# Edge items held behind the middle stage on DVE and ACT, and the diagonal written from another queue: a four-layer graph network on one core

## The chip, the cores and the metric

The kernel runs on one core of a Trainium2 chip. The metric is the device time of one execution in microseconds; the time before is the median of three runs. A core has five engines with a queue each: TensorE (PE, with its weight loads PEld), VectorE (DVE), ScalarE (ACT), GpSimd (POOL) and SyncE (SP). SP issues DMA transfers alone; POOL issues the indirect ones (gathers and scatters by a list of indices) and some plain ones.

## The reference, cut to what matters

32 graphs of 512 nodes with 256 features go through four layers, all in float32. The adjacency matrix is shared by all graphs and sparse: a bernoulli mask of 1/128, made symmetric, with the diagonal set.

```python
# layers 0 and 3, with weights of their own
hidden = relu(pre_u[:, :, None, :] + pre_v[:, None, :, :] + b1)      # pre_u = h W1[:d], pre_v = h W1[d:]
S = sigmoid(einsum('buvk,ko->buvo', hidden, W2)[..., 0] + b2[0])
a_t = einsum('buv,bud->bvd', S * A_a, h_t)
m_t = einsum('uv,bud->bvd', A_m, h_t) * h_t
z_t = beta1 * h_t + beta2 * (a_t Wa + ba) + beta3 * (m_t Wm + bm)
# layer 1
z + relu((A z) W^T + b)
# layer 2
feats = data W1^T;  f1 = feats W2 + b2
coefs = softmax(leaky_relu(f1_i + f1_j) + bias1)                     # bias1 is the adjacency matrix
coefs feats + bias2 + data
```

S is needed only where the adjacency matrix is not zero: at the edges and on the diagonal.

## The kernel before

**Groups, edges and items.** Where no node has too many neighbours (the case here), `sparse_path` runs. The 32 graphs are taken in 8 groups of four (`NB`). For layers 0 and 3 the edges are packed beforehand into 36 lists of 128 edges (`ITEMS`), the same for all graphs. For each group and each of the two layers, a table in DRAM holds pre_u and pre_v of all nodes for the four graphs (`pre`, L547 to L555 write it: L547 adds the bias out of PSUM, L548 copies the other half on ACT, L550 and L551 make the diagonal's sums `self_s`, SP stores the result at L555). An edge stage (`edges`) then works through the 36 items: POOL gathers 128 rows of the table (`fetch`, L580, "rows<-table,iv"), SP or POOL brings the rows of the other end of the edges ("mine", L620 or L580), DVE adds the two (L652) and makes four reductions, one per graph (L665), into `s`. Every four items ACT takes exp (`exp_of`, L565), and DVE finishes the sigmoid and multiplies by the edge's value (`sigmoid_of`, L569 and L570, then L609). POOL scatters each finished list into `cells` in DRAM (`put`, L574), two halves of the matrix in turn; a scatter into a half waits for the one before it into that half. The diagonal (`own_1`) gets its exp after item 2 and its sigmoid after item 4, L600 multiplies it by the diagonal of the matrix, and POOL writes it into `cells` (L604). A stage fetches three items ahead (five at the program's ends) into five row buffers.

**The middle stage.** When a group's edge stage of layer 0 is through, four loads on POOL (`load`, L690) bring the cells back as SA, and `middle` takes the four graphs one after the other through the rest of layer 0 (L772 copies SA to `flat`; L713 mhT; L803 and L810 on PE, L808 and L811 give zT), layer 1 (L823 zW, L829 and L830 yT) and layer 2 (L841 feats, L845 fcol, L848 the transposes into f; the softmax in L856 to L862, its transposes L901 and the copies L902; L879 adds the result to yT), and then through layer 3's `pre`, which fills the table for layer 3's edge stage. When that has run, `last` makes the group's output (L703, L713, L943, L950, L959, L962).

**What sets the order.** `weave` writes the pieces of all stages of all groups into one list. Each stage is a generator, each `yield` ends a piece, and each piece has a due time in units of a group's period, set by hand in `sparse_path`; pieces are recorded in the order of their times. The stages overlap: while group t is in its middle stage, layer 3's edge stage of group t-1 runs in the first half of the period and layer 0's edge stage of group t+1 in the second half, and pieces of kind "fill" (`first`, which makes layer 0's table, and `last`) are put between the middle's pieces where these leave room. The recorded order is not the final one. When the program is built, a scheduler goes through it with its own estimate of durations, and on each engine it may put an instruction ahead of one recorded before it, if by that estimate the operands are there earlier. The order that it arrives at is fixed in the program; on the chip, DVE, ACT, POOL and SP work through their queues in it, and an instruction that waits holds up all behind it.

Of the kernel before, what the change touches and what calls it, by code (L numbers as in the profile page):

```python
# [11 lines left out]
AF = mybir.ActivationFunctionType  # L12
ALU = mybir.AluOpType
# [34 lines left out]
class Model:  # L48


    def __init__(self, ctx, tc, a):
        nc = self.nc = tc.nc
        self.tc, self.a = tc, a
        const = self.const = ctx.enter_context(tc.tile_pool(name="const", bufs=1))
        self.ident = const.tile([P, P], F32, name="ident")
        make_identity(nc, self.ident)
        self.adj = const.tile([P, NC, N], F32, name="adj")
        for c in range(NC):
            nc.sync.dma_start(self.adj[:, c, :], a["adj"][c * P : (c + 1) * P, :])
        self.g0, self.g3 = self.gnn_first("L0_gnn"), self.gnn_first("L3_gnn")  # L60
# [354 lines left out]
class Sparse:  # L415
# [3 lines left out]
    def __init__(self, ctx, m, counts, xr, outr, B):  # L419
        self.m, self.nc, self.tc, self.counts = m, m.nc, m.tc, counts  # L420
        tc = m.tc
        self.xr, self.outr = xr, outr
        pool = lambda n, b, **k: ctx.enter_context(tc.tile_pool(name=n, bufs=b, **k))
        self.dram = pool("dram", 1, space=bass.MemoryType.DRAM)

        self.cells = {
            k: [self.dram.tile([CELLS + SPARE, NB], F32, name=f"cells_{k}{q}") for q in range(2)] for k in "03"
        }
        self.lists = self.dram.tile([N, 2 * N], F32, name="lists")
        self.x2s = self.dram.tile([B, P, NC, D], F32, name="x2s")  # L430

        self.xT, self.x2T = (self.dram.tile([B, P, DC, N], F32, name=n) for n in ("xT", "x2T"))
        self.e = Edges(m, pool("edges", 1))
        self.adjT = pool("adjT1", 1).tile([P, NC, N], F32, name="adjT")
        self.grp = pool("grp", 2)
        self.act, self.small, self.gath = pool("act", 1), pool("small", 2), pool("gath", 5)
        self.ps = pool("ps", 7, space=PSUM)
        self.ps_f1 = pool("ps_f1", 1, space=PSUM)
        self.later, self.bigs, self.given = None, 0, None

    def psum(self):
        return self.ps.tile([P, N], F32, name="pst", tag="pst")
# [1 line left out]
    def weave(self, streams):  # L444

        order = []
        for k, (_, times, _) in enumerate(streams):
            order += [(at, k, j) for j, at in enumerate(times)]  # L450
        due, running = [], set()

        def run(k, j):
            g, times = streams[k][:2]
            room = next(g, None)
            if j == len(times) - 1:
                for _ in g:
                    raise AssertionError("more pieces than told")
            return room

        def fill(upto):
            while len(due) > upto:
                run(*due.pop(0))

        for _, k, j in sorted(order):
            kind, end = streams[k][2], len(streams[k][1]) - 1
            if kind == "fill":
                due.append((k, j))
                fill(HELD if running else 0)
                continue  # L470
            if kind == "main" and j == 0:
                running.add(k)
            elif j == 0 and kind != "free":
                fill(0)
            if run(k, j) and due:
                fill(len(due) - (1 if len(due) < HELD // 2 else 2))
            if kind == "main" and j == end:
                running.remove(k)
        fill(0)

    def big(self, dtype, n, layer=None):

# [79 lines left out]
        self.later = None  # L562

    def exp_of(self, w, t):
        self.nc.scalar.activation(t, t, AF.Exp, bias=w["nb2"], scale=-1.0)  # L565

    def sigmoid_of(self, t):

        self.nc.vector.tensor_scalar(t, t, 1.0, None, ALU.add)  # L569
        self.nc.vector.reciprocal(t, t)  # L570

    def put(self, g, half, at, s):
# [11 lines left out]
    def edges(self, g, spare=()):  # L584

        nc, e, w = self.nc, self.e, g.w
        flat = "p c b -> p (c b)"
        own = g.self_s.rearrange(flat)  # L590
        ready, fetched = [], {}
        lead = LEAD_AT_ENDS if spare else LEAD
        tags = [None] * 5 + list(spare)
        mine = {}
        places = g.table.rearrange("(c p k) n -> c k p n", p=P, k=2)

        def own_1():
            self.sigmoid_of(own)
            diag = self.counts.diag.unsqueeze(2).to_broadcast([P, NC, NB])
            nc.vector.tensor_tensor(g.self_s, g.self_s, diag, ALU.mult)  # L600
            for q in range(2):
                diagonal = g.cells[q][q * HALF : q * HALF + HALF * (N + 1), :]
                diagonal = diagonal.rearrange("(c p a) b -> p c a b", p=P, a=N + 1)[:, :, 0, :]
                nc.gpsimd.dma_start(diagonal, g.self_s[:, 2 * q : 2 * q + 2, :])  # L604

        def run_1(ks):
            self.sigmoid_of(g.s[:, ks, :].rearrange(flat))
            value = e.value[:, ks].unsqueeze(2).to_broadcast([P, ks.stop - ks.start, NB])
            nc.vector.tensor_tensor(g.s[:, ks, :], g.s[:, ks, :], value, ALU.mult)  # L609
            for k in range(ks.start, ks.stop):  # L610
                j = e.order[k]
                ready.append((e.half_of(j), e.cell[:, j : j + 1], g.s[:, k, :]))

        def fetch(n):
            j = e.order[n]
            c = j // OWN
            if c >= NC or c not in mine:
                t = self.gath.tile([P, GROUP], F32, name="mine", bufs=3)
                if c < NC:
                    nc.sync.dma_start(t, places[c, 0])  # L620
                    mine[c] = t
                else:
                    self.fetch(t, g, e.iu[:, j - NC * OWN : j - NC * OWN + 1])
            else:
                t = mine[c]
            if tag := tags[n % len(tags)]:
                rows = self.act.tile([P, GROUP], F32, name="rows_more", tag=tag)
            else:
                rows = self.gath.tile([P, GROUP], F32, name="rows")
            self.fetch(rows, g, e.iv[:, j : j + 1])  # L630
            fetched[n] = rows, t

        def put():

            at = next((n for n, r in enumerate(ready) if r[0] != self.half), 0)
            if ready:
                r = ready.pop(at)
                self.half = r[0]
                self.put(g, *r)

        self.half = 1
        for n in range(lead):
            fetch(n)
            yield

        todo = [(2, lambda: self.exp_of(w, own)), (4, own_1)]
        done = 0
        for k in range(ITEMS):
            for _ in range(2 if spare and len(ready) > 2 else 1):
                put()  # L650
            rows, other = fetched.pop(k)
            nc.vector.tensor_tensor(rows, rows, other, ALU.add)  # L652
            if k + lead < ITEMS:
                fetch(k + lead)
            if spare:
                by_entry = rows.rearrange("p (b d) -> p b d", b=NB)
                w2 = w["W2bc"].unsqueeze(1).to_broadcast([P, NB, D])
                nc.vector.scalar_tensor_tensor(by_entry, by_entry, 0.0, w2, ALU.max, ALU.mult)
            for b in range(NB):
                part = rows[:, b * D : (b + 1) * D]  # L660
                at = g.s[:, k, b : b + 1]
                if spare:
                    nc.scalar.activation(part, part, AF.Identity, accum_out=at)
                else:
                    nc.vector.scalar_tensor_tensor(part, part, 0.0, w["W2bc"], ALU.max, ALU.mult, accum_out=at)  # L665
            if k % 4 == 3 or k >= ITEMS - 3:
                ks = slice(done, k + 1)
                near = spare or k >= ITEMS - 5
                todo.append((k + (1 if near else 3), lambda ks=ks: self.exp_of(w, g.s[:, ks, :].rearrange(flat))))
                todo.append((k + (1 if near else 4), lambda ks=ks: run_1(ks)))  # L670
                done = k + 1
            while todo and todo[0][0] <= k:
                todo.pop(0)[1]()
            yield
        for _, f in todo:
            f()
        for _ in range(TAIL - 1):
            put()
            yield
        while ready:  # L680
            put()
        yield
# [629 lines left out]
```

## Time and profile before

| | us |
|---|---|
| median of three runs | 3211.44 |
| the runs | 3209.15, 3211.44, 3216.03 |
| the profiled execution | 3218.37 |
| its span in the trace | 3216.7 |

| engine | busy us | share of the span | instructions |
|---|---|---|---|
| PE | 2740.0 | 85% | 8646 |
| DVE | 2344.3 | 73% | 7594 |
| POOL | 1526.4 | 47% | 1344 |
| ACT | 976.4 | 30% | 2309 |

The mean granted clock of TensorE is 0.927 of full speed. A group is told by its start on the timeline; one engine's busy time in a stretch, in the windows view, stands next to the stretch's length. A line of a timeline reads: start, duration, engine, source line, operation, tile written <- tiles read, shapes, count, and in brackets the idle time of the engine in front of it and what ended it. "pst" is any PSUM tile of the main pool, which has seven banks; L45 is the helper that makes one product from several matmuls, so that its groups are told apart by their tiles. In a line of the waits view stand the waiting instruction, what it waited for, the sum, the number of waits, and the longest.

### The profile page before, as it was taken

The page shows a single profiled execution, that of the slowest core. Times are in us where ns is not written, and L with a number is a line of the kernel's source. Part 1 is how long each engine was busy: PE and PEld are TensorE (multiplying, and loading weights), DVE is VectorE, ACT ScalarE, POOL GpSimd, SP SyncE. Part 2 cuts the span into 40 slices and gives each one's busy share as a digit, 9 for nine tenths or more (in the row PEclk, how much of TensorE's full clock was granted, in tenths as well). Part 3 has the DMA queues.
Part 4 walks back from the last instruction along what each step waited for, and adds up shares of the span by engine and source line. Part 5 has one row for each costly group of instructions (what it writes and reads, how often), then busy time and mean ns, then how long its engine had stood idle before and what let it go on. Part 6 is the DMA issues. An engine that isn't in the chain of part 4 may idle for free.

```text
span 3216.7 us, 32210 instructions
## 1 busy us (share of the span) xinstructions
PE 2740.0 (85%) x8646; PEld 1646.8 (51%) x8646; DVE 2344.3 (73%) x7594; ACT 976.4 (30%) x2309; POOL 1526.4 (47%) x1344
## 2 busy tenths in 40 slices
PE   6357798889996999979996999969999799889947
PEld 3233444456543565436653565436654466546626
DVE  6777838987796959868596876968598785952661
ACT  3453333322132222312232222322223122232440
POOL 1565505555453635556255554636355562620461
PEclk9678989999998999989998999989999899999968
DMA  8876437776687657765677666876578656631653
GB/s 286 285 250 227 158 120 235 255 255 205 208 263 233 210 177 231 262 202 192 213 236 234 209 210 191 266 237 208 178 225 267 209 191 210 221 134 46 210 190 111
DMA packets 295036, 679.37 MB, mean 211 GB/s; under 512 B 44992, under 2 KB 163264, under 8 KB 286656
## 3 DMA queue, kind: packets, MB, share of 16 engines
q0 software_dynamic: 121408, 406.15, 39.3%
q1 hardware_dynamic: 154480, 233.88, 21.8%
q10 hardware_dynamic: 18960, 37.24, 3.2%
q8 instruction: 70, 1.15, 0.1%
q14 instruction: 118, 0.97, 0.1%
HBM read 531.12 MB, written 146.01 MB: 211 GB/s over the span
## 4 chain that ended last, share of the span: by engine, by line
PE 36%; DVE 31%; DMA 21%; issue 6%; ACT 3%; POOL 2%; SPq 0%; POOLq 0%; ACTq 0%; DVEq 0%
PE pst L45 25%; DVE rows L665 10%; DVE rows L652 10%; DMA rows<-table,iv 6%; DMA table<-puv 5%; DMA cells<-s,cell 4%; PE pst L950 4%; PE pst L959 2%; PE pst L803 2%; DMA mine<-table,iu 2%; PE pst L901 2%; DVE ex L857 1%; ACT flat L772 1%; DVE mhT L713 1%; POOL rows L580 1%
## 5 line engine op out<-in xcount | busy, mean ns | idle before, releaser
L574 POOL DMA_INDIRECT cells<-s,cell x576 | 677.9, 1177 | 592.6 <-DMA cells<-s,cell 379.7
L580 POOL DMA_INDIRECT rows<-table,iv x554 | 664.9, 1200 | 553.4 <-DVE rows L665 246.0
L652 DVE TENSOR_TENSOR rows<-rows,mine 128x1024 f32<-128x1024 f32 x554 | 667.4, 1215 | 299.2 <-DMA rows<-table,iv 286.2
L665 DVE SCALAR_TENSOR_TENSOR rows<-rows,L_gnn_W2bc 128x256 f32<-128x256 f32 x2016 | 749.6, 414 | 0.2
L45 PE MATMUL pst<-adj,h 128*128 128x512 f32 x1024 | 452.4, 592 | 0.0
L45 PE MATMUL pst<-L_gnn_Wa,hT 128*128 128x256 f32 x1024 | 266.4, 413 | 121.9 <-DMA hT<-xT 59.2
L45 PE MATMUL pst<-w_L_gnn_W,yT 128*128 128x512 f32 x512 | 239.0, 622 | 84.8 <-DVE yT L879 84.8
L45 PEld LDWEIGHTS pst<-adj,h 128*128 128x128 f32 x1024 | 192.3, 190 | 217.1 <-issue 214.3
L45 PEld LDWEIGHTS pst<-L_gnn_Wa,hT 128*128 128x128 f32 x1024 | 209.2, 210 | 169.7 <-issue 52.6
L45 PE MATMUL pst<-w_L_gnn_W,hT 128*128 128x512 f32 x512 | 251.6, 629 | 13.6 <-ACT hT L535 12.0
L45 PE MATMUL pst<-eT,feats 128*128 128x512 f32 x512 | 232.2, 607 | 11.5 <-ACT eT L902 11.5
L45 PE MATMUL pst<-adjT,zW 128*128 128x512 f32 x512 | 224.9, 592 | 0.0
L548 ACT COPY puv<-pst 128x256 f32<-128x256 f32 x256 | 94.5, 371 | 409.0 <-DVE puv L547 396.3
L950 PEld LDWEIGHTS pst<-hWa,SA 128*128 128x128 f32 x896 | 212.8, 328 | 5.7 <-issue 3.3
L950 PE MATMUL pst<-hWa,SA 128*128 128x256 f32 x896 | 215.0, 397 | 0.0
L45 PEld LDWEIGHTS pst<-w_L_gnn_W,yT 128*128 128x128 f32 x512 | 101.6, 200 | 212.7 <-issue 108.7
L45 PE MATMUL pst<-WT,hT 128*128 128x256 f32 x512 | 148.4, 447 | 61.1 <-DVE hT L811 60.9
L803 PE MATMUL pst<-flat,hWa 128*128 128x512 f32 x448 | 196.8, 592 | 0.0
L604 POOL DMA_DIRECT2D cells<-self_s x32 | 24.0, 758 | 361.1 <-DVE self_s L600 220.5
L565 ACT ACTIVATE s<-s,L_gnn_nb 128x16 f32<-128x16 f32 (+2 forms) x176 | 53.7, 306 | 462.2 <-DVE rows L665 461.7
L772 ACT COPY flat<-SA 128x512 f32<-128x512 f32 x128 | 134.7, 1126 | 180.7 <-PE pst L45 107.4
L901 PE MATMUL pst<-ident,ex 128*128 128x128 f32 x512 | 90.6, 317 | 98.8 <-DVE ex L862 61.5
(167 smaller groups left out, 3801.7 us busy)
## 6 DMA issues: line engine op xcount, KB each, us to landing
table<-puv SPq DMA_DIRECT2D x256, 256.0 KB, 5.6
SA<-cells POOLq DMA_DIRECT2D x64, 1024.0 KB, 7.3
h<-in_x_dram SPq DMA_DIRECT2D x64, 512.0 KB, 5.9
mine<-table SPq DMA_DIRECT2D x64, 512.0 KB, 7.2
hT<-xT SPq DMA_DIRECT2D x36, 512.0 KB, 3.7
h<-x2s SPq DMA_DIRECT2D x36, 512.0 KB, 3.9
xT<-hT ACTq DMA_DIRECT2D x32, 512.0 KB, 8.6
x2T<-yT SPq DMA_DIRECT2D x32, 512.0 KB, 5.2
```

The lines of the kernel that those rows point to most:

```text
L45: nc.tensor.matmul(out, lhsT, rhs, start=(n == 0), stop=(n == len(pairs) - 1))
L548: nc.scalar.copy(puv[:, 1, :], pp[:, D:])
L565: self.nc.scalar.activation(t, t, AF.Exp, bias=w["nb2"], scale=-1.0)
L574: self.nc.gpsimd.indirect_dma_start(out=g.cells[half], out_offset=bass.IndirectOffsetOnAxis(ap=at, axis=0), in_=s, in_offset=None)
L580: self.nc.gpsimd.indirect_dma_start(out=rows, out_offset=None, in_=g.table, in_offset=bass.IndirectOffsetOnAxis(ap=at, axis=0))
L652: nc.vector.tensor_tensor(rows, rows, other, ALU.add)
L665: nc.vector.scalar_tensor_tensor(part, part, 0.0, w["W2bc"], ALU.max, ALU.mult, accum_out=at)
L772: self.nc.scalar.copy(flat[:, r, :], SA[r][:, :, b])
L803: nc.tensor.matmul(pz, hWa[:, r, cs], flat[:, r, :], start=(r == 0), stop=False)
L901: nc.tensor.transpose(pt[:, js], ex[:, js], self.m.ident)
L950: nc.tensor.matmul(pz[:, k * D : (k + 1) * D], SA[r][:, cs, b], hWa[:, r, :], start=(r + k == 0), stop=False)
L959: nc.tensor.matmul(pz[:, k * D : (k + 1) * D], mhT[:, d, cs], w["Wm"][:, d, :], start=False, stop=(k * d == 1))
```

## The change

Three things are done. `weave` notes, after each piece of the middle stage, the last instruction recorded on each engine of interest (`mark`). `behind` gives an instruction an ordering dependency, without a semaphore, on the instruction noted last but one on its engine, so that the scheduler cannot put it ahead of that one; it is called for an item's add on DVE, for every exp of the edge stages on ACT and for the first step of every sigmoid on DVE. And the diagonal is written by SP instead of POOL.

```diff
@@ Sparse.__init__
-        self.later, self.bigs, self.given = None, 0, None
+        self.later, self.bigs, self.given, self.marks = None, 0, None, {}
@@ weave
-            if run(k, j) and due:
+            room = run(k, j)
+            if kind == "main":
+                self.mark()
+            if room and due:
                 fill(len(due) - (1 if len(due) < HELD // 2 else 2))
@@ new functions
+    def last_of(self, engine):
+        for i in reversed(self.nc.cur_bb.bb.instructions):
+            if i.engine == engine:
+                return i.name
+
+    def mark(self):
+        for engine, names in self.marks.items():
+            names.append(self.last_of(engine))
+
+    def behind(self, ins):
+        names = self.marks.setdefault(ins.ins.engine, [])
+        if len(names) > 1 and names[-2]:
+            order = mybir.DependencyInfo(mybir.DependencyClass.NoSync, mybir.DependencyReason.DATA)
+            self.tc.add_manual_dep(ins.ins, names[-2], order, reason="behind the middle stage")
@@ exp_of
-        self.nc.scalar.activation(t, t, AF.Exp, bias=w["nb2"], scale=-1.0)
+        self.behind(self.nc.scalar.activation(t, t, AF.Exp, bias=w["nb2"], scale=-1.0))
@@ sigmoid_of
-        self.nc.vector.tensor_scalar(t, t, 1.0, None, ALU.add)
+        self.behind(self.nc.vector.tensor_scalar(t, t, 1.0, None, ALU.add))
@@ own_1
-                nc.gpsimd.dma_start(diagonal, g.self_s[:, 2 * q : 2 * q + 2, :])
+                nc.sync.dma_start(diagonal, g.self_s[:, 2 * q : 2 * q + 2, :])
@@ edges, the item's add
-            nc.vector.tensor_tensor(rows, rows, other, ALU.add)
+            self.behind(nc.vector.tensor_tensor(rows, rows, other, ALU.add))
```

## The prediction

> **What bounds the kernel now.** I read the page's chain first (PE 36%, DVE 31%, DMA 21%), which names no single engine, then the windows view. From about 716 to 2839 us the trace repeats every 374 to 376 us, one group of four graphs, and each of the four graphs' middle passes starts its softmax with four transposes into f (L848). In PE's timeline they start at 2011.6, 2098.8, 2199.8, 2292.1 and 2386.7; I call the four stretches A, B, C and D.
>
> ```profile
> core 0: us, PE busy (x) PEld busy (x) DVE busy (x) ACT busy (x) POOL busy (x), PEclk, DMA share, GB/s
> 2011.60:2098.80 87.20, 81.57 (x246) 42.19 (x245) 82.24 (x305) 31.49 (x68) 51.49 (x46) 0.98 0.80 265
> 2098.80:2199.80 101.00, 76.35 (x221) 43.11 (x220) 68.33 (x230) 23.98 (x48) 47.76 (x42) 0.86 0.68 218
> 2199.80:2292.10 92.30, 88.42 (x301) 57.76 (x300) 70.70 (x249) 25.28 (x49) 51.89 (x47) 0.98 0.61 200
> 2292.10:2386.70 94.60, 90.19 (x310) 59.34 (x309) 66.96 (x209) 22.82 (x43) 35.62 (x32) 0.98 0.61 198
> ```
>
> A is bound by DVE (82.2 of 87.2 us busy), C and D by PE. B is bound by neither: PE is busy for 76 of 101 us, DVE for 68. The waits view of PE over B says for what it waits:
>
> ```profile
> PE pst L45 <- DVE yT L879: 15.7, 1, 15.7
> PE pst L45 <- DVE hT L811: 4.4, 1, 4.4
> PE pst L901 <- DVE ex L862: 3.8, 2, 2.6
> PE pst L45 <- ACT eT L902: 0.7, 1, 0.7
> ```
>
> The timelines of PE, DVE and POOL around that wait:
>
> ```profile
> 2038.86 7.03 PE L45 MATMUL pst<-w_L_gnn_W,yT 128*128 128x512 f32 x16
> ...
> 2114.72 7.13 PE L45 MATMUL pst<-eT,feats 128*128 128x512 f32 x16 [0.73 <-ACT eT L902]
> 2137.53 9.29 PE L45 MATMUL pst<-w_L_gnn_W,yT 128*128 128x512 f32 x16 [15.68 <-DVE yT L879]
> ```
> ```profile
> 2110.32 0.49 DVE L862 TENSOR_SCALAR ex<-ex,cols 128x512 f32<-128x512 f32 x1
> 2131.33 1.22 DVE L652 TENSOR_TENSOR rows<-rows,mine 128x1024 f32<-128x1024 f32 x1 [20.52 <-DMA rows<-table,iv]
> ...
> 2136.73 0.74 DVE L879 SCALAR_TENSOR_TENSOR yT<-pst,col_L_gnn_bias,yT 128x512 f32<-128x512 f32 x1
> ```
> ```profile
> 2121.07 0.97 POOL L574 DMA_INDIRECT cells<-s,cell  x1 [3.87 <-DMA cells<-s,cell]
> ...
> 2124.65 1.00 POOL L580 DMA_INDIRECT rows<-table,iv  x1 [0.36 <-issue]
> ```
>
> DVE executes in order. Its queue holds three items (L652) of a new edge stage ahead of L879, the middle stage's next step; the first item's rows are fetched only at 2124.65, behind the old stage's last scatters on POOL, so DVE stands still for 20.5 us and PE for 15.7 us although L879's input was ready at 2121.6. The same wait stands in five groups (18.5, 18.0, 17.9, 15.7, 14.7 us in PE's waits by group).
>
> **The change, part by part.** I compared the two built kernels' orders. PE's order is the same but for 133 instructions moved by at most six places; SP has 32 more transfers, POOL 32 fewer. On DVE an item of these groups stood up to 49 places ahead of where the program recorded it; now nearly all stand within ten. No instruction is added on the compute engines. Items between one softmax start (L845) and the next, before and after: A 19, 21; B 19, 19; C 17, 20; D 17, 12. An item costs DVE 2.5 us: one add (L652, two take 2.35 us, 1.14 apart) and four reductions (L665, 0.35 apart in the timeline).
>
> *B.* L879 now stands ahead of the new stage's first item, so the wait on L879 (15.7) can go; L811 stood behind the late items and loses its 4.4. Slow matmuls after the two long waits go with them: 16 took 9.29 where 16 of the same take 7.03 (2.3 us), and 16 on hT took 6.22 where the same take 3.62 at 1886 (2.6 us). I leave the softmax wait (3.8) and the eT wait. Removed: 15.7 + 4.4 + 2.3 + 2.6 = 25.0. Put back: the old stage's last four items, which stood ahead of the softmax, now stand between it and L879. DVE was free at 2110.8; 4 x 2.5 + 1 us of small sigmoid work ends at 2121.8, two L879 at 0.65 at 2123.1, against PE's readiness at 2121.6: 1.5 us. The first rows fetch now has only four of the tail's scatters ahead of it, yet still waits for the table's last write (mine loads, which need it too, were issued at 2114.7), and I add one item's length, 2.5, for rows that come that late. B: -25.0 + 4.0 = -21.0. Ends: -27 (nothing put back, half of the softmax wait gone), and -5 if only L811's wait is spared.
>
> [...]
>
> *A.* Two more items in the stretch that DVE bounds: +5.0. Ends 0 (DVE's 5.0 us of idle absorb them) and +6.
>
> *C.* Three more items are 7.5 us on a DVE with 21.6 us idle, and PE bounds: 0. Ends -3.9 (C's one PE wait, on L862) and +7.5.
>
> *D.* Five fewer items. D holds the other boundary: the last graph's pass ends, the next edge stage begins, and its first items stood ahead of both mhT steps (L713) and L811. They now stand behind L713, and three ahead of L811: PE's waits on these (3.2 + 1.2 = 4.4) go, 4.0 taken. Ends -6.1 (1.7 more: behind such waits fourteen matmuls on hT took 4.97 us at 1977.84, where fourteen took 3.29 at 2070.10) and +24.6, the rival below. The last item (number 35) moves behind the last softmax; its 2.5 us are covered by 7.5 us of PE fill work (L950) in front of the transposes. If that cover were gone, 2.5 us more.
>
> *Exponentials on ACT.* They follow their items. In B those of the last items now stand ahead of the four flat copies (L772), which start about 2.5 us later; PE has 7 us of work before it needs them. 0; at worst +2.5.
>
> *Diagonal on SP.* POOL loses two issues of 0.75 us per edge stage and the wait in front of them:
>
> ```profile
> 1921.13 1.14 POOL L690 DMA_DIRECT2D SA<-cells  x2 [1.71 <-ACT ex L856]
> 1951.68 1.44 POOL L604 DMA_DIRECT2D cells<-self_s  x2 [29.41 <-DVE self_s L600]
> 1955.82 1.04 POOL L580 DMA_INDIRECT rows<-table,iv  x1 [2.70 <-issue]
> ```
>
> The wait looks large, 29.4 us, but what is behind it, the next stage's fetches, needs a table whose last write lands at 1953.1 by the chain: 0, at best -2.7 per D. On SP it waits for item 5's neighbourhood in DVE's order; behind it stand one mine load (wanted some 15 items later) and the next graph's hT, which waits for L830 anyway: 0. [...]
>
> *Sum.* A group: -21.0 + 5.0 + 0 - 4.0 = -20.0; five groups: -100. The group before them (521.8 to 882.4) has no L879 wait; PE waits 8.2 us on L811 and 7.4 on L862 in its B, and I take half, -8. In the first group 34 items instead of 24 fall into three passes in which DVE idles for 50 us: 0. The last pass and the final edge stage (2839 to 3217) keep their order: 0. Total -108. The profiled execution took 3218.4 (span 3216.7), 6.9 above the median of the runs, 3211.4. 3218.4 - 108 = 3110, on the median's footing 3103.
>
> **Rivals.** *All of PE's waits go.* DVE then runs A at 87, B at 75 (68.3 plus a wait of 6.4 on a table write), PE runs C at 88 and D at 90: 340 instead of 375, so -35 x 5 - 16 = -191: 3020; with half of the surplus over mine, 3050. For: the new order follows the order in which PE delivers. Against: A is bound by DVE, and softmax steps wait on each other.
>
> *The wait only moves.* Item 0's rows still come late, and L547 and L811, now behind items 0 to 6, stand in L879's place. B then gains only some 10 (15.7 + 2.3 less the items put back and L811's wait grown by 4), a group -9 at A's price: 3160. For: the fetch still shares POOL with the scatters. Against: only four of the tail's scatters remain ahead of it.
>
> *The tail of the edge stage comes late: slower.* Place: L772, L803 at the end of D. Item 35 moves from 1896 to about 1928.5 in this trace's time. If everything behind it takes as long as in B before (from 2096.5 to SA's last landing at 2147.5, 51 us), SA lands at 1979.5, flat is copied by 1983.7 and PE wanted it at 1959.1: +24.6 a group in place of -4, so -21 + 5 + 24.6 = +9; six groups give 3260. It decides against the change once SA lands 21 us late or more. Against: in B the last SA load stood behind seven fetches; in D it took 33 us from item 35, which means 6.6 us late, and now only one scatter is left after item 35.
>
> *The order does not bite.* Excluded by the built order but for a gain that cancels: 3211.
>
> **How the numbers follow.** Forecast (3065 to 3150) 0.53; all waits go (3015 to 3065) 0.15; the wait moves (3150 to 3200) 0.17; no change 0.03; late tail (3215 to 3280) 0.12. The range 3035 to 3200 holds the forecast, the moved wait and two thirds of the first rival: 0.80. Faster 0.53 + 0.15 + 0.17 = 0.85, same 0.03, slower 0.12; 0.2%, 6.4 us, is about what a measurement of this kernel can tell.
>
> **What would show it.** Right: in B PE's wait on L879 under 4 us and B near 80 us; A near 92 and still DVE-bound; POOL no longer waiting on self_s; D without PE waits on L713 or L811. Wrong: a DVE wait on rows that a middle step stands behind, of 10 us or more; PE waiting on flat (L772) at L803; the group longer than 370 us.

## The result, and the profile after

| | before | after |
|---|---|---|
| median us | 3213.74 | 3161.34 |
| profiled execution us | 3218.37 | 3165.21 |
| its span us | 3216.7 | 3163.5 |
| ratio, with its 95% interval | | 0.9835 (0.981 to 0.986) |

The medians are of four executions of each kernel, timed together. The changed kernel is 52 us faster, within the range given (3035 to 3200) and on the side forecast, but with under half of the forecast gain of 108 us. In the trace the span is 53.2 us shorter. Measured from softmax start to softmax start on PE, and averaged over the five groups of the forecast's sum, it comes from here (us):

| | before | after | change | forecast |
|---|---|---|---|---|
| ahead of the first softmax | 284.6 | 292.7 | +8.1 | 0 |
| first group | 237.3 | 236.4 | -0.9 | 0 |
| second group | 360.6 | 365.3 | +4.7 | -8 |
| A | 87.5 | 89.0 | +1.5 | +5 |
| B | 103.2 | 93.6 | -9.6 | -21 |
| C | 90.8 | 86.9 | -3.9 | 0 |
| D | 94.2 | 93.6 | -0.6 | -4 |
| a group (A to D) | 375.7 | 363.0 | -12.7 | -20 |
| last pass and end | 455.9 | 454.0 | -1.9 | 0 |

Most line numbers are 22 higher in the changed kernel: L879 is now L901, L811 is L833, L830 is L852, L862 is L884, L845 is L867, L652 is L674, and on POOL the scatter is L596 and the gather L602. Some kernels of the experiments differ from these by one to three. The windows view of the changed kernel for A, B, C and D of the group that was shown of before (columns: window, length, then busy time and instructions of PE, PEld, DVE, ACT and POOL, granted clock, DMA share, GB/s):

```profile
1990.38:2077.09 86.71, 81.04 (x247) 42.66 (x245) 80.32 (x285) 29.85 (x63) 45.83 (x39) 0.98 0.75 245
2077.09:2171.12 94.03, 76.41 (x221) 44.03 (x220) 77.03 (x272) 25.51 (x52) 53.39 (x48) 0.89 0.78 256
2171.12:2257.97 86.85, 86.85 (x302) 56.52 (x301) 74.56 (x254) 24.86 (x48) 52.77 (x45) 1.00 0.65 206
2257.97:2352.83 94.86, 90.93 (x309) 59.77 (x308) 57.67 (x177) 23.60 (x46) 30.80 (x30) 0.96 0.63 200
```

C has become what PE needs: busy for all of its 86.85 us at full clock. B still has 17.6 us in which PE is idle (24.7 before), and PE is busy there for 76.4 us, as before, with as many instructions. What PE waits for in this B, by the waits view (in total, times, longest):

```profile
PE pst L923 <- DVE ex L884: 7.5, 2, 6.7
PE pst L45 <- DVE hT L833: 6.6, 2, 5.8
PE pst L45 <- DVE yT L852: 2.8, 1, 2.8
PE pst L45 <- ACT eT L924: 0.7, 1, 0.7
```

The 15.7 us on L879 are gone. But the wait on the softmax has gone from 3.8 to 7.5, the one on hT, which the forecast struck out, from 4.4 to 6.6, and one on yT (2.8) is new. These four differences are -7.0 us together, which is what this B got shorter (101.0 to 94.0). The places in the timelines of PE, DVE and POOL of the changed kernel:

```profile
2077.09 0.60 PE L870 MATMUL f<-ident,feats 128*128 128x128 f32 x4
...
2087.80 1.09 PE L923 MATMUL pst<-ident,ex 128*128 128x128 f32 x4 [6.68 <-DVE ex L884]
...
2104.62 7.03 PE L45 MATMUL pst<-w_L_gnn_W,yT 128*128 128x512 f32 x16
...
2137.22 1.22 PE L45 MATMUL pst<-WT,hT 128*128 128x256 f32 x2 [5.79 <-DVE hT L833]
2139.20 4.69 PE L45 MATMUL pst<-WT,hT 128*128 128x256 f32 x14 [0.76 <-DVE hT L833]
...
2159.18 4.08 PE L45 MATMUL pst<-WT,yT 128*128 128x257 f32 x10 [2.83 <-DVE yT L852]
```
```profile
2082.47 0.22 DVE L867 TENSOR_SCALAR fcol<-feats,twob 128x4 f32<-128x4 f32 x1
...
2135.34 1.23 DVE L674 TENSOR_TENSOR rows<-rows,mine 128x1024 f32<-128x1024 f32 x1 [5.92 <-DMA rows<-table,iv]
2136.48 0.68 DVE L833 TENSOR_TENSOR hT<-hT,pst 128x512 f32<-128x512 f32 x1
```
```profile
2121.28 1.00 POOL L596 DMA_INDIRECT cells<-s,cell  x1 [4.24 <-DMA cells<-s,cell]
...
2126.69 1.01 POOL L596 DMA_INDIRECT cells<-s,cell  x1 [3.84 <-DMA cells<-s,cell]
2128.01 1.14 POOL L602 DMA_INDIRECT rows<-table,iv  x1 [0.30 <-DVE self_s L592]
```

Two chains are read here. *The handover on POOL* (from the old edge stage to the new one). The add at 2135.34 is item 6 of the new edge stage; it stands ahead of L833. Its rows are fetched at 2128.01, behind two scatters of the old stage that each waited some 4 us for an earlier scatter to land. DVE stands for 5.92 us, PE for 5.79, and 14 matmuls behind that take 4.69 us. *The softmax.* The transposes into f start at 2077.09, but DVE comes to fcol only at 2082.47, as the last adds and reductions of A, and table steps between them, are still in front of it, and the first transpose of ex follows 10.7 us after f. In the kernel before, DVE had done fcol ahead of f:

```profile
2097.01 0.23 DVE L845 TENSOR_SCALAR fcol<-feats,twob 128x4 f32<-128x4 f32 x1
```
```profile
2098.84 0.60 PE L848 MATMUL f<-ident,feats 128*128 128x128 f32 x4
...
2104.13 0.63 PE L901 MATMUL pst<-ident,ex 128*128 128x128 f32 x4 [1.26 <-DVE ex L862]
```

There 5.3 us lay between the two. So the extra items of A, forecast as +5.0 in A, were, by this reading, mostly paid at B's softmax, whose first transpose of ex comes 5.4 us later behind f than before; the half-width run below bears on it.

### The profile page after: what moved, and what is told of

Same layout as the page of the kernel before. It is cut to its first block, busy times and chain, and to the rows that moved or that the text cites. A ratio compares the mean times of both kernels' runs of the same rounds, so it can differ in the third digit from the quotient of the medians.

```text
span 3163.5 us, 32203 instructions
## 1 busy us (share of the span) xinstructions
PE 2734.3 (86%) x8645; PEld 1650.1 (52%) x8646; DVE 2357.2 (75%) x7594; ACT 977.2 (31%) x2309; POOL 1468.5 (46%) x1312
## 5 line engine op out<-in xcount | busy, mean ns | idle before, releaser
L602 POOL DMA_INDIRECT rows<-table,iv x554 | 631.8, 1140 | 874.6 <-DVE rows L687 211.6
L596 POOL DMA_INDIRECT cells<-s,cell x576 | 671.1, 1165 | 625.7 <-DMA cells<-s,cell 422.4
L674 DVE TENSOR_TENSOR rows<-rows,mine 128x1024 f32<-128x1024 f32 x554 | 669.1, 1217 | 154.6 <-DMA rows<-table,iv 143.0
L687 DVE SCALAR_TENSOR_TENSOR rows<-rows,L_gnn_W2bc 128x256 f32<-128x256 f32 x2016 | 740.9, 418 | 2.1
L45 PE MATMUL pst<-w_L_gnn_W,hT 128*128 128x512 f32 x512 | 245.2, 617 | 8.4 <-ACT hT L557 6.0
L45 PE MATMUL pst<-WT,hT 128*128 128x256 f32 x512 | 166.8, 486 | 93.3 <-DVE hT L833 92.7
L45 PE MATMUL pst<-eT,feats 128*128 128x512 f32 x512 | 232.0, 607 | 10.6 <-ACT eT L924 10.0
L45 PE MATMUL pst<-w_L_gnn_W,yT 128*128 128x512 f32 x512 | 226.5, 594 | 1.0 <-DVE yT L901 1.0
L825 PE MATMUL pst<-flat,hWa 128*128 128x512 f32 x448 | 196.8, 592 | 0.0
L45 PEld LDWEIGHTS pst<-WT,hT 128*128 128x128 f32 x512 | 121.8, 247 | 142.7 <-DVE hT L833 117.2
L569 DVE TENSOR_TENSOR puv<-pst,bc_L_gnn_b 128x256 f32<-128x256 f32 x256 | 104.2, 415 | 87.8 <-DMA table<-puv 48.0
L45 PEld LDWEIGHTS pst<-eT,feats 128*128 128x128 f32 x512 | 96.8, 193 | 127.1 <-issue 109.5
```

What stands on the lines that cost most here:

```text
L45: nc.tensor.matmul(out, lhsT, rhs, start=(n == 0), stop=(n == len(pairs) - 1))
L569: nc.vector.tensor_tensor(puv[:, 0, :], pp[:, 0:D], w["b1bc"], ALU.add)
L596: self.nc.gpsimd.indirect_dma_start(out=g.cells[half], out_offset=bass.IndirectOffsetOnAxis(ap=at, axis=0), in_=s, in_offset=None)
L602: self.nc.gpsimd.indirect_dma_start(out=rows, out_offset=None, in_=g.table, in_offset=bass.IndirectOffsetOnAxis(ap=at, axis=0))
L674: self.behind(nc.vector.tensor_tensor(rows, rows, other, ALU.add))
L825: nc.tensor.matmul(pz, hWa[:, r, cs], flat[:, r, :], start=(r == 0), stop=False)
```

## The experiments

Ratios are to the kernel before, timed on the same chip in the same session; group times are means over the same five groups of the profiled execution, waits are from the group of the views above unless said otherwise. The first four ask which part of the change carries the gain.

**The diagonal alone.** The kernel before with one edit:

```diff
-                nc.gpsimd.dma_start(diagonal, g.self_s[:, 2 * q : 2 * q + 2, :])
+                nc.sync.dma_start(diagonal, g.self_s[:, 2 * q : 2 * q + 2, :])
```

> The kernel before with the diagonal written by SyncE and nothing else. VectorE's order is nearly that of before (the first items of the new edge stage still stand ahead of L879). Theory O (the gain is VectorE's order alone, and the diagonal costs at the start): L879's wait stays at 14 to 18 us per group, the groups keep 375 us, the first softmax comes some 8 us later than the 284.6 us of before, and the total is about 3219. Rival D (the diagonal off GpSimd gives part of the gain, the 3.9 us of C): groups of 371 us or less, total 3190 to 3195.

Ratio 0.9971 (0.9952 to 0.9989), groups of 372.7 us, first softmax at 288.2. PE's waits by line, over the whole execution:

```profile
PE pst L45 <- DVE yT L879: 99.4, 6, 20.9
```

The wait that the change is about stays (84.8 us in five pieces before), so the diagonal alone does not touch it. It does bring a little, 0.3%: less than rival D's 20 to 25 us, but not the zero of the forecast, and C stays at 92.0 us.

**The order alone.** The changed kernel with the diagonal on POOL again.

> The changed kernel with the diagonal written by GpSimd again, as before: the orders of TensorE, VectorE and ScalarE are those of the changed kernel, only GpSimd and SyncE differ. Theory O: the groups take the changed kernel's 363 to 364 us, the first softmax comes at about 285 us instead of 292.7, total about 3153. Rival D: C goes back from 86.9 to about 91 us, groups of 368, total about 3185; the first softmax stays at 292 to 293 if the order of the items is what made it late.

Ratio 0.9848 (0.9818 to 0.9879), groups of 364.3 us (A 89.3, B 95.9, C 86.8, D 92.4), first softmax at 288.8. C keeps its 86.8 us: its gain belongs to the order. That the diagonal adds anything on top of the order (0.9835 against 0.9848) can't be told with these intervals.

**The first six items alone.** The order for the adds of items 0 to 5 only, no exps or sigmoids, diagonal on POOL:

```diff
-            self.behind(nc.vector.tensor_tensor(rows, rows, other, ALU.add))
+            add = nc.vector.tensor_tensor(rows, rows, other, ALU.add)
+            if k < 6:
+                self.behind(add)
```

> The kernel before with an order for the first six items of each edge stage only (their add stands behind the middle stage's last piece but one); the later items and all exponentials run as far ahead as the scheduler likes, and GpSimd writes the diagonal. The old stage's last four items stand ahead of the softmax again, as before. Theory O in its narrow form (all of the gain is L879 no longer standing behind the first three items): PE's wait on L879 under 3 us in B, B at about 94, total 3150 to 3165. Rival W (the other items' order carries half of it: C's and L811's waits): L879's wait gone, but L811's at 10 us or more, C at 90 or more, total 3180 to 3195.

Ratio 0.9833 (0.98 to 0.9866): as much as the whole change, in other places: A 99.4, B 90.6, C 87.4, D 87.5, together 364.9. Theory O in its narrow form holds for the total, as does its reason (L879's wait in B is 2.3 us). What differs is A, 11.9 us longer than before. DVE's longest wait in that A and PE's, in the group of the other views:

```profile
DVE rows L674 <- DMA mine<-table,iu: 6.3, 1, 6.3
```
```profile
PE pst L925 <- DVE ex L886: 6.7, 1, 6.7
```

The two lie at opposite ends of A. The 6.7 us are at A's own softmax, which has items in front of it. The 6.3 us come at the end, where the old stage's panel items, which have both operands gathered by POOL, come late; there PE waits 4.5 us for L572, a table step that stands behind the late add. So the later items' order is not idle: it spares A 10.4 us and costs B and D 9.1.

**One piece tighter.** Behind the last piece of the middle stage (names[-1] in place of names[-2]).

> The changed kernel with the order one piece tighter: behind the middle stage's last piece instead of its last but one. One or two more of the old stage's last items go behind L879, and each later item stands about one place later. Theory O: the distance matters little, 3150 to 3175, as the first items are behind L879 either way. Rival L (VectorE has no slack in A and at the softmax, so each place counts): a softmax that starts earlier in B, PE's wait on ex there under 4 us instead of 6.7, and 10 us or more less in all; or, if items then come late for SA, a wait on flat (L825) and 10 us or more longer.

Ratio 0.9849 (0.9821 to 0.9878): the total is that of the change. Inside it, the groups take 358.9 us, 4 less, and the first group, with 251.7 us instead of 236.4, uses up most of that. Rival L's sign, a shorter wait at B's softmax, isn't there (6.8 us in total in that B).

The next group asks what B's remaining idle time is. All three kernels leave work out, as their expectations say.

**Reductions of half width.**

```diff
-                    nc.vector.scalar_tensor_tensor(part, part, 0.0, w["W2bc"], ALU.max, ALU.mult, accum_out=at)
+                    part, w2h = part[:, : D // 2], w["W2bc"][:, : D // 2]
+                    nc.vector.scalar_tensor_tensor(part, part, 0.0, w2h, ALU.max, ALU.mult, accum_out=at)
```

> The changed kernel with each item's four reductions (L687) reading only half of their columns: 288 reductions a group of 0.418 us become shorter, some 0.15 us each, 43 us of VectorE a group, and the scores are partial sums. Theory V (A is full on VectorE, so B's softmax starts late): PE's wait on ex in B under 2 us instead of 6.7, A at 83 or less, groups of 350 or less instead of 363, total 3085 or less. Rival G (what remains is GpSimd's queue: an item's rows come late whatever VectorE has left): VectorE only waits longer for rows, groups of 357 or more, total 3130 or more.

Ratio 0.9605 (0.9576 to 0.9634), groups of 352.6 us (A 86.4, B 89.0, C 86.6, D 90.6). Between the two theories: DVE has 35 us less work in a group (254.5 us against 289.6 in the group of the views), and 10.4 us of the group go. At B's softmax, DVE comes to fcol about 1 us ahead of f in all five groups, where in the changed kernel it came 4.7 to 5.4 us behind, with the same number of items between one softmax and the next. Five table steps of some 0.35 us, which the built order now has behind fcol, are under 2 us of that; the rest is DVE's shorter work on items. But theory V's own sign, a wait on ex under 2 us, is not there: PE's first transpose of ex follows f by 7.3 us on average (10.4 in the changed kernel, 5.3 before), and in the group of the views PE waits 4.9 us for the second, whose steps stand behind a table step on which DVE waits 2.2 us for an earlier write of the table.

**No tail scatters.**

```diff
-                ready.append((e.half_of(j), e.cell[:, j : j + 1], g.s[:, k, :]))
+                if spare or k < ITEMS - 6:
+                    ready.append((e.half_of(j), e.cell[:, j : j + 1], g.s[:, k, :]))
```

> The changed kernel without the scatters of the last six items of each edge stage but the first and the last (those cells keep what stood there), so that the new stage's fetches on GpSimd have no waiting scatters ahead of them. Theory G: PE's wait on hT (L833) under 2 us in B and in D instead of 6.6 and 3.9, and the slow matmuls behind it gone, B near 84, D near 88, groups near 350, total near 3095. Rival V: B's wait on ex stays at 6 us or more and hT's wait shrinks little as VectorE is late there in any case, groups of 358 or more, total 3135 or more.

Ratio 0.9608 (0.9584 to 0.9631), groups of 350.0 us (A 88.7, B 86.9, C 86.8, D 87.6): close to theory G's figures. DVE's built order is that of the changed kernel, so what differs is POOL's queue and the scatters' own transfers. POOL's and PE's timelines of this kernel at the places shown above (L834 here is L833 there):

```profile
2046.21 0.94 POOL L602 DMA_INDIRECT rows<-table,iv  x1 [0.30 <-DVE rows L675]
...
2048.05 1.05 POOL L602 DMA_INDIRECT rows<-table,iv  x1 [0.30 <-issue]
```
```profile
2066.84 0.70 PE L45 MATMUL pst<-WT,hT 128*128 128x256 f32 x2 [0.67 <-DVE hT L834]
2068.82 3.29 PE L45 MATMUL pst<-WT,hT 128*128 128x256 f32 x14 [1.28 <-DVE hT L834]
```

The fetches go out with no wait on a scatter between them, the wait on hT falls from 5.79 to 0.67 us and the 14 matmuls behind it from 4.69 to 3.29; in D no wait on hT is left. The wait on ex stays at 7.3 us in B: the softmax is a cost of its own.

**Both left out.**

> Half-width reductions and no tail scatters together, on the changed kernel. If VectorE's load at the softmax (theory V) and GpSimd's queue at the handover (theory G) are two separate costs, their gains add: group 363 - 10.4 - 13.0 = 339.6, B near 82 (the figure of the forecast), total 3030 to 3050. If they are one chain seen twice (the rows come late because VectorE freed the buffers late, or the other way round), the group stays at 345 to 350, B at 86 or more, total 3065 to 3090.

Ratio 0.9428 (0.9411 to 0.9446). The windows view, A to D:

```profile
1901.21:1987.16 85.95, 79.73 (x246) 41.41 (x245) 74.98 (x304) 30.03 (x64) 50.05 (x44) 1.00 0.78 249
1987.16:2070.98 83.82, 74.66 (x222) 43.01 (x220) 63.66 (x255) 25.29 (x51) 41.23 (x38) 0.94 0.83 279
2070.98:2157.61 86.63, 86.63 (x301) 56.68 (x300) 64.42 (x254) 24.91 (x48) 51.43 (x49) 1.00 0.66 214
2157.61:2245.41 87.80, 87.80 (x310) 58.45 (x309) 51.41 (x177) 23.49 (x46) 21.23 (x19) 1.00 0.64 215
```

Groups of 344.2 us: 18.8 less than the changed kernel, where the two alone gave 10.4 and 13.0, so four fifths of the sum. The two costs are mostly separate; in C and D PE is now busy throughout, so that there was no more to gain there. B is 83.9 us on average; the forecast had it at 82.2. So the two together account for 9.7 of the 11.4 us by which B missed the forecast.

The rest looks for a version that keeps all work and gets this time.

**The old stage's tail held too.** The first-six kernel with `if k < 6 or (k >= ITEMS - 5 and w is self.m.g3)`.

> The run with the order for the first six items, plus the same order for the last five items of the layer-3 edge stages (those of the boundary in B), which in that run stood ahead of B's softmax and made A 99.4 us long. By the theory that each place where an item stands ahead of a middle step that is ready costs what the trace shows, A goes from 99.4 to 88, B from 90.6 to 92, C and D stay at 87.5: groups near 355, total near 3115. By the rival that the groups are held by something else (a bound of all orders near 363, as three orders gave 363 to 365), the 11 us of A come back as waits in B, groups 361 to 366, total 3150 to 3170.

Ratio 0.988 (0.9859 to 0.9901), A 100.4, groups of 367.0. The edit did not do what was meant: in the trace only one of the stage's last four items stands behind the softmax. Three still stand ahead of it, the first of them ahead of the yT step L854 too; its panel rows come 8.2 us late, and PE waits 8.5 us for L854. It says nothing for or against a common bound.

**Five fetches ahead** (LEAD 5 instead of 3).

> The changed kernel with five rows fetches ahead of an edge stage's first item instead of three; all else by its own order. Theory G: item 5's and 6's rows are there when wanted, hT's wait in B under 3 us instead of 6.6, in D under 2, groups near 354, total near 3110. Rival V: hT's wait shrinks, the softmax wait stays, and as all five rows buffers are then held by fetches, a fetch waits for the item that still uses its buffer: groups 361 to 368, total 3150 to 3180.

Ratio 0.9858 (0.9836 to 0.988), groups of 365.7. In B the wait on hT falls from 6.6 to 2.4 us and that on yT rises from 2.8 to 6.6; DVE waits 11.7 us for rows as before (12.0). The lateness moves to the next step. So the number of fetches in front is not what is short; that it is POOL's time at the handover fits this, and rests on the run without tail scatters.

**Halves in turn.** Items in an order in which consecutive scatters always go to different halves of cells:

```diff
-        order = [item_of(0, j) for j in range(OWN // 2)]
...
-            order += tail[j : j + 1]
+        order = [item_of(c, j) for j in range(OWN) for c in (0, 2)]
+        for j in range(OWN):
+            order += [item_of(1, j), item_of(3, j)]
+            if j in (4, 6):
+                order += [panel_of(h, j // 2 % PANELS) for h in range(2)]
```

> The changed kernel with another order of the 36 items within an edge stage, all work kept: blocks 0 and 2 in turn, then 1 and 3, with the four panel items in pairs after the 26th and 32nd, so that consecutive scatters always go to different halves of cells; in the changed kernel the first four items all scatter into one half, and four of the last five into the other, each behind the landing of the one before. Theory G: GpSimd's wait on earlier scatters at the handover shrinks, rows come earlier, hT's wait in B under 3 us instead of 6.6 and D near 88, groups 350 to 356, total 3095 to 3125. Rival: a half takes one scatter per landing in any case, so the waits only spread over the stage, and SA's loads for the first half start later as its last items stand later: groups 361 to 368, total 3150 to 3180.

Ratio 1.0001 (0.9986 to 1.0016): the whole gain is gone. In B the wait on hT is 0.9 us, as theory G has it, and B is 91.2; but A takes 97.6, C 90.3 and D 94.6, and the last pass and end 18.4 us more. POOL's waits on earlier scatters did shrink; this is the line of the changed kernel, then that of this one, then the costliest of DVE's waits in this one:

```profile
POOL cells L596 <- DMA cells<-s,cell: 422.4, 171, 6.5
```
```profile
POOL cells L593 <- DMA cells<-s,cell: 229.8, 124, 5.9
```
```profile
DVE rows L671 <- DMA mine<-table,iu: 140.7, 29, 11.8
```

DVE waits 140.7 us on the panel items' second gather, against 11.1 in the changed kernel. So the time saved on scatters was lost, at least in part, on panels.

**Halves in turn with the first-six order.**

> The run with the order for the first six items only, with the items' order of halves in turn. There A lost 11 us to items at the end of the stage that stand ahead of B's softmax (a panel item's mine rows came 6.3 us late behind GpSimd's scatters), and D was at its 87.6. Theory G: the panels come earlier and the last scatters wait less, so A goes from 99.4 to 90 or less with B, C and D as they were (90.6, 87.4, 87.5): groups near 355, total near 3110. Rival: A keeps 96 or more, as the two blocks' items still end ahead of the softmax; groups 361 to 368, total 3150 to 3180.

Ratio 0.9837 (0.982 to 0.9854), groups of 361.7: D is 87.5 as theory G has it and B, with 85.0, better, but A is 98.6 and C 90.6. The rival's figures hold: A keeps its items, and in it DVE still waits 7.5 us on the panels' second gather.

**The panels' order turned** (`for h in (1, 0)` in place of `for h in range(2)`).

> The changed kernel with the panel items of the second half ahead of those of the first, so that of each stage's last eight scatters the first five go into one half and the last four alternate, where in the changed kernel the last four go into one half. Theory G: two landings less to wait for at the handover: hT's wait in B from 6.6 to about 3, in D from 3.9 to 2, groups near 357, total near 3130. Rival: the row of scatters into one half only stands four items earlier, the last ones come as late as before, and SA's loads of the first half start later: groups 361 to 366, total 3150 to 3170.

Ratio 0.9933 (0.9909 to 0.9957), slower than the change by about 1%: groups of 369.1, and DVE's wait for rows in B is 13.6 to 14.7 us in the two groups looked at, against 12.0. Scatters still wait between the fetches (4.58 us for the one ahead of a fetch at 2134.28). Both expectations were wrong here, the rival's too; why it is that much slower was not settled.

**The change from the third group on.** A counter of middle stages begun; order and SP's diagonal only where it is over 2:

```diff
-        if len(names) > 1 and names[-2]:
+        if self.middles > 2 and len(names) > 1 and names[-2]:
...
-                nc.sync.dma_start(diagonal, g.self_s[:, 2 * q : 2 * q + 2, :])
+                (nc.sync if self.middles > 2 else nc.gpsimd).dma_start(diagonal, g.self_s[:, 2 * q : 2 * q + 2, :])
```

> The changed kernel with its order and SyncE's diagonal from the third group's middle stage on only; before that everything stands as in the kernel before. Theory S (where no long wait stands, the order and the diagonal only cost: 8.1 us ahead of the first softmax and 4.7 us in the second group): first softmax at 283 to 287, second group 360 to 362, later groups 363, total about 3148. Rival N (the start scatters from profile to profile by as much): first softmax anywhere from 284 to 293, total 3155 to 3170.

Ratio 0.9804 (0.9777 to 0.983). The first softmax starts at 289.0 us, with the same order up to there as the kernel before, whose profile had 284.6: 4.4 of the 8.1 us can be scatter from profile to profile, as rival N has it. The second group takes 358.4 instead of 365.3. That price was real: of the kernels that do all work with the items in their own order, those with the whole or the tighter order in that group take 363.8 to 367.2 us there, those without any order there 353.6 to 360.6. Both theories are half right; that the kernel is faster than the change (0.9804 against 0.9835) can't be told with these intervals.

**The tighter order from the third group on.** The same with names[-1].

> The tighter order (behind the middle stage's last piece) and SyncE's diagonal from the third group on only. Theory S: the groups keep the 358.9 us that the tighter order had, and the 25 us that it lost ahead of the third group are not paid: total about 3134. Rival T (the loss is the price of turning from one order to the other and is paid wherever that falls): the third group takes 375 us or more, total 3150 to 3170.

Ratio 0.9744 (0.9717 to 0.9771), 3134.82 us median: faster than both kernels, and theory S's total, though the groups are not the 358.9 that it rests on. First group 237.5, second 353.6, the next five 360.5 on average (B still 93.9). The 15 us that the tighter order lost in the first group are not paid at the third (361.4 us), so rival T falls.

**Both together**, this and the panels turned.

> The tighter order from the third group on with the panels turned. If both theories hold: groups near 353, total near 3105. If only the start's does: 3134. If neither: 3150 to 3170.

Ratio 0.9798 (0.9771 to 0.9825), groups of 360.0, as without the turn. What turning the panels costs lies outside these groups: the first softmax is 4.2 us later, and the first group (245.3), the second (358.2) and the end are each longer by 5 to 8 us, in the one profile of each. Why was not settled.

## Why the prediction was wrong by half

*What bounds the kernel: right.* L879 behind items whose rows are late was the wait to remove. It fell to 2.3 us or less, in the B shown, in every kernel that held the first items back, and ordering six items of 36 was worth the whole change. The size, though, is that of the rival *the wait only moves*, which had 3160 us and a chance of 0.17 against 0.53, and so is the mechanism: L833 (L811 in the prediction) behind items 0 to 6 stands in L879's place. Only it is item 6's rows that come late there, not item 0's.

*B, -21.0 forecast, -9.6 measured: the step that failed.* It is the sentence "L811 stood behind the late items and loses its 4.4", with the 4.9 us of slow matmuls that were to go along and the single 2.5 us put back for late rows. The new items stand ahead of L833 as they stood ahead of L879 (items 0 to 6 now, 0 to 2 then), and each of their fetches shares POOL's queue with the old stage's scatters. The forecast priced only the first fetch ("only four of the tail's scatters ahead of it"); item 6's came behind two that waited 4.24 and 3.84 us. Leaving the tail's scatters out gave 6.7 us of B back. PE's busy time in the B shown did not fall at all (76.4 us): by the clock records it worked 13.1 us at half clock, behind the new waits, and 12.8 before, behind the old ones. The miss in this B, 14.0 us (-7.0 instead of -21.0), adds up by terms: hT 6.6 (4.4 that did not go and 2.2 more), slow matmuls 4.9, softmax 3.7, yT 2.8, less the 4.0 that the forecast put back.

*A, +5.0 forecast, +1.5 measured: the mechanism right, the place wrong.* DVE's surplus came out as a softmax whose transposes start 5.4 us later, and that was in B, where the forecast left the softmax wait at its 3.8. Counting items from fcol to fcol and time from f to f hid this. A and B together were forecast at -16.0 and gave -8.1. With half-width reductions fcol came ahead of f again and A and B lost 7.2 us: that DVE is short there is shown. How much of the 7.5 us on ex is due to it is not: 4.9 stayed.

*C, 0 forecast, -3.9 measured.* The lower end of its bounds: two adds stood between fcol and the first step on ex of C's softmax and now stand elsewhere, and PE's one wait in C is gone. The order alone does it (86.8). The forecast did not see this gain; without it, a group would have gained 9 us, so part of the half that came is luck.

*D, -4.0 forecast, -0.6 measured.* The same error as in B: L833 still waits for rows (PE 3.9 us in D of the group shown), as the handover to the next stage lies here. Without tail scatters D took 87.6, 6.6 less than before, a little past the bound of -6.1.

*Second group, -8 forecast, +4.7 measured.* The forecast halved the waits that it saw there. Without a wait on L879 the order had little to remove and cost instead; left out there, the group took 358.4 us. The order of the first six items alone did not cost there (354.4).

*First softmax, 0 forecast, +8.1 measured.* About half can be scatter; what the rest is stays open.

*The diagonal, 0 forecast.* Alone it gave 0.3%; with the order nothing that these runs can tell. As forecast, POOL no longer waits on self_s to write it (220.5 us before), and as forecast that was hardly worth time.

*The rivals.* The late tail did not come: no wait on flat (L825) grew into the groups; its whole is 13.0 us, 11.0 of it at the first middle stage, against 10.6 before. *All waits go* had 3015 to 3065 us; the run with both costs left out, which does less work, gave 3036. Of the prediction's signs, the wait on L879 and POOL's on self_s went as it says; B near 80 and a D without a wait on L811 did not come, and none of the signs of being wrong did: in the five groups DVE's longest wait for rows is 7.5 us, though there are several.

## What to carry to other kernels

In an in-order queue, taking an instruction out of the way of one step puts it in the way of the next (in B, PE's 15.7 us on L879 went, and its wait on L833 grew from 4.4 to 6.6): price the wait again at every step that the moved work now stands ahead of, and follow the late input back to its own queue. A gain that rests on moving late work is bounded by why the work is late; the cheap test is to leave the suspected work out and see which wait goes. An order that pays in the steady state can cost where the wait it removes doesn't stand, so switch it on from there: the tighter order gave 0.9849 throughout and 0.9744 from the third group on.

## What the runs showed of the hardware

In the changed kernel matmuls were slow behind a wait of under 3 us too: at 2159.18, behind one of 2.83 us, ten took 4.08 us, where four of the same took 1.03 at 2166.53 (2.6 for ten). The granted clock, in the column before the last two, was 0.50 where they started:

```profile
2155.72:2159.13 3.41, 0.62 (x3) 0.19 (x1) 3.41 (x15) 0.00 (x0) 2.80 (x3) 1.00 0.19 52
2159.13:2162.54 3.41, 3.37 (x8) 2.73 (x9) 3.38 (x12) 0.75 (x2) 1.98 (x2) 0.50 0.89 290
2162.54:2165.95 3.41, 3.41 (x11) 1.80 (x10) 3.36 (x11) 0.58 (x2) 2.18 (x2) 1.00 0.44 163
```

In the 3.41 us ahead of these matmuls PE was busy for 0.62 us. A wait cut into shorter ones did not bring the clock back here: with waits of up to 6.7 us in B, where the longest had been 15.7, B's granted clock went only from 0.86 to 0.89.

Halving the width of the reductions did not halve their cost here: the 288 of 256 columns (a mean of 0.418 us) kept DVE busy for 106.7 us in the group of the views of the changed kernel, and with 128 columns all of DVE's work in such a group was 35 us less (254.5 us against 289.6).
